# Releasing the row scatters of two slots together, behind one TensorE product

## The chip, the cores and the metric

The kernel runs on one core of a Trainium2 chip. The metric is the device time of one execution in microseconds (us). The core has five engines, each with its own in-order instruction stream: TensorE (PE; its weight loads are listed as PEld), VectorE (DVE), ScalarE (ACT), GpSimd (POOL) and SyncE (SP, which here only issues DMAs). They wait for one another through semaphores. Every DMA, whoever issues it, runs on the same 16 DMA engines.

## The reference

One layer of message passing on a graph of 6,250 nodes and 100,000 edges, 128 features each. For every edge, the features of its source node, of its destination node and of the edge itself go through one linear layer, a layer norm and a ReLU; the messages are summed per source node, added to the node's features, and the sum is normalised.

```python
row, col = (edge_index[0], edge_index[1])
msg_in = jnp.concatenate([x[row], x[col], edge_attr], axis=-1)
h = msg_in @ W + b
mu = jnp.mean(h, axis=-1, keepdims=True)
var = jnp.mean(jnp.square(h - mu), axis=-1, keepdims=True)
h = (h - mu) * jax.lax.rsqrt(var + LN_EPS) * gamma + beta
msg = jax.nn.relu(h)
out = jax.ops.segment_sum(msg, row, num_segments=x.shape[0])
# and outside: x = _layernorm(x + out)
```

Edges come sorted by destination. The sum goes by source, which is in no order.

## The kernel before, in words

The kernel sorts the edges by blocks of source nodes through device memory. The 100,000 edges are 782 tiles of 128, and four tiles are a **slot** (196 slots, numbered q). In each slot PE multiplies the edge features (L611) and adds the rows of the destination nodes, which it picks out of a small window with a one-hot matrix (L615). ACT moves the four finished tiles from PSUM into one of eight buffers `hs` (L623; slot q uses buffer q mod 8) and adds the source's number within its block (L624). POOL then writes the 128 rows of each tile to their places in a table `sorted` in device memory, with one indirect DMA per tile (L641): four **scatters** per slot, 782 in all.

The tiles are cut into six **splits** (42, 42, 42, 30, 20 and 20 slots), each with a table of its own. While the slots of one split run, the table of the split before is read back, two blocks of 125 nodes at a time (a **pair**, SP's loads `hl`, L715), and worked off in steps that are woven into the slots by a fixed flow (`FLOW`, `work`): DVE builds the one-hot matrix (`ohe`, L733), PE turns it (L745) and ACT copies it (L749), ACT seeds PSUM with the rows (L755), PE adds the source rows (L772), ACT squares and takes roots (L781, L784), DVE scales (L790, L796), PE sums by node (L805), DVE adds to the accumulator (L810). The last split has a loop of its own at the end (class `Unit`, loads L831, one-hot L838). Ahead of all this, some 42 slots also project the node features (L391 to L417), and `places` works out where each row goes.

The order of PE, DVE, ACT and SP is written out by hand. POOL has its own stream, which in this stage holds scatters alone. A slot's scatters are collected in the list `waiting`. Up to slot 12 and from slot 195 on they are issued untied, as soon as ACT has written the buffer. Between, `scatters(n, True)` is called in each slot and takes the n = 4 scatters of the slot before; `done` lists the products that PE was given since the last call with their costs (4 for an f32 product, 1 for a bf16 one), and the loop over `done` picks those at which 1/4, 2/4, 3/4 and 4/4 of the cost is reached. Scatter k waits by semaphore for product `at[k]`. So the four scatters of slot q - 1 go out along the products of slot q. Each scatter also waits until the scatter eight before it has landed, since there are eight semaphores for them.

What depends on a scatter: ACT's write of the same `hs` buffer eight slots later, and the first `hl` load of a split, some five slots after the split's last slot; for the last split that is the first load at L831.

Of the kernel before, what the change touches and what calls it, by code (L numbers as in the profile page):

```python
# [84 lines left out]
def fast_path(ctx, tc, io, bad_d, found):  # L85
# [10 lines left out]
    written = mybir.DependencyInfo(mybir.DependencyClass.Sync, mybir.DependencyReason.DATA)  # L96
# [91 lines left out]
    iota_p, zero_p, at = beside[:, 0:P], beside[:, P:P + 1], beside[:, P + 8:P + 8 + NB]  # L188
# [27 lines left out]
    def more_constants():  # L216
        nc.vector.tensor_copy(ident_f16, ident)
        nc.vector.tensor_scalar(minus_f16, ident, -1.0, None, op0=ALU.mult)
        nc.vector.tensor_scalar(twice_f16, ident, 2.0, None, op0=ALU.mult)
# [342 lines left out]
    def edge_loads(q):  # L562

        if q % DG or q >= PIECES:
            return
        t0 = q * PT
        g = min(DG, PIECES - q)
        if ("eT", q // DG) not in held:
            edge_feats(q)
        db = edge.tile([P, DG * PT * P], BF16, name="db", bufs=3)  # L570
        if q >= BY_PE:
            c1 = g * PT * P
            nc.sync.dma_start(
                db[:, :c1], dram_ap(drel_d, t0 * P, [[0, P], [1, c1]]))
        held[q // DG] = (held.pop(("eT", q // DG)), db)

    def edge_window(q):
        if q >= PIECES:
            return
        k = sum(q >= x for x in TABLE_FROM[1:])  # L580
        base = nc.values_load(base_c[0:1, q:q + 1], engines=[mybir.EngineType.SP],
                              min_val=0, max_val=TABLES[k][1] - TABLES[k][0] - WN,
                              skip_runtime_bounds_check_because="kept inside the table")
        win = edge.tile([P, D], BF16, name="win", bufs=6)
        i = nc.sync.dma_start(win[:3 * WN, :], xb_d[k][:, bass.ds(base, WN), :])
        held["win", q] = win
        return i

    def edge_hot(q):
        if q >= PIECES:  # L590
            return
        m = min(PT, TILES - q * PT)
        c0 = q % DG * PT * P
        db = held[q // DG][1][:, c0:c0 + m * P]
        if q < BY_PE:
            db = psum.tile([P, PT * P], F32, name="sel", bufs=BANKS["sel"])
            nc.tensor.matmul(db, ones_h[0:1, :], drel0[0:1, q, :], start=True, stop=True)
        oh = edge.tile([P, PT * P], BF16, name="ohd", bufs=3)
        nc.vector.tensor_scalar(oh[:, :m * P], db, part_w, None, op0=ALU.is_equal)  # L599
        held["oh", q] = oh  # L600

    def edges(s, q):
        t0 = q * PT
        m = min(PT, TILES - t0)
        c0 = q % DG * PT * P
        eT = held[q // DG][0][:, c0:c0 + m * P]
        oh, win = held.pop(("oh", q)), held.pop(("win", q))
        hp = psum.tile([P, PT, P], F32, name="hp", bufs=2)
        for j in range(m):
            at = slice(j * P, (j + 1) * P)  # L610
            pe(nc.tensor.matmul(hp[:, j, :], eT[:, at], w[:, 2, :], start=j == 0, stop=False,  # L611
                                skip_group_check=True), 4)
        for j in range(m):
            at = slice(j * P, (j + 1) * P)
            pe(nc.tensor.matmul(hp[:, j, :], oh[:3 * WN, at], win[:3 * WN, :],  # L615
                                start=False, stop=j == m - 1, skip_group_check=True))
        held["hp", q] = hp

    def evict(s, q):
        t0 = q * PT  # L620
        m = min(PT, TILES - t0)
        hs, hp = hs_all[q % HS], held.pop(("hp", q))
        nc.scalar.copy(hs[:, :m, 0:D], hp[:, :m, :])  # L623
        nc.scalar.copy(hs[:, :m, D], sloc[:, t0:t0 + m])  # L624
        waiting.extend((s, q, j) for j in range(m))

    TIE = (12, 195)
    waiting = []

    def scatters(n, tied):  # L630

        total, seen, at = sum(c for _, c in done), 0, []
        for i, c in done:
            seen += c
            while len(at) < n and seen * n >= (len(at) + 1) * total:
                at.append(i)
        done.clear()
        for k, (s, q, j) in enumerate(waiting[:n]):
            t = q * PT + j
            parts = P if t < TILES - 1 else LAST  # L640
            i = nc.gpsimd.indirect_dma_start(  # L641
                out=sorted_d[s][:, :],
                out_offset=bass.IndirectOffsetOnAxis(ap=place_i[:parts, t:t + 1], axis=0),
                in_=hs_all[q % HS][:parts, j, :], in_offset=None,
            )
            if tied:
                tc.add_manual_dep(i.ins, at[k].name, written, reason="rows behind products")
            tc.declare_no_dep(i.ins, group=f"scatter{s}", reason="rows of different edges")
            tc.add_to_no_dep_group(f"scatter{s}", i.ins)
            if q < EARLY:  # L650
                tc.declare_no_dep(i.ins, group="clear", reason="see check_early")
                tc.add_to_no_dep_group("early", i.ins)
        del waiting[:n]
# [305 lines left out]
    def run(g, n=1):  # L959
        for _ in range(n):  # L960
            next(g, None)
# [114 lines left out]
    def work(n):  # L1076

        nonlocal n_steps
        for _ in range(n):
            for off, step in FLOW:  # L1080
                i = n_steps - LEAD - off
                if i % 4 or not 0 <= i // 4 < len(pairs):
                    continue
                if step is None:
                    load_pair(*pairs[i // 4])
                    continue
                if off == 0:
                    at_work[i // 4] = Pair(*pairs[i // 4])
                step(at_work[i // 4])
            n_steps += 1  # L1090
# [7 lines left out]
    def steps_due(q):  # L1098
        for (q0, n0), (q1, n1) in zip(due, due[1:]):
            if q0 <= q < q1:  # L1100
                return n0 + (n1 - n0) * (q - q0) // (q1 - q0)
        return 0
# [3 lines left out]
    def clear_pairs(s, n):  # L1106
        for p0 in range(cleared[s], min(cleared[s] + n, NB // 2)):
            i = clear(s, p0, 1, nc.sync)
            if s == 0:
                tc.declare_no_dep(i.ins, group="early", reason="see check_early")  # L1110
                tc.add_to_no_dep_group("clear", i.ins)
            cleared[s] = p0 + 1

    ahead = 3
    for s, (n_tiles, _, _, _) in enumerate(SPLITS):
        p0, p1 = first_tile[s] // PT, -(-first_tile[s + 1] // PT)
        slots = p1 - p0
        for i in range(slots):
            q = p0 + i
            for g in groups:  # L1120
                run(g)
            if q == 1:
                more_constants()

            while ahead <= min(q + 4, 3 + q + q // 3):
                edge_loads(ahead)
                edge_window(ahead)
                ahead += 1
            if s + 1 < n_split and i >= slots - (30 if s else 26):
                clear_pairs(s + 1, 1 if slots > NB // 2 else 2)  # L1130
            edge_hot(q + 2)
            edges(s, q)
            for g in groups:
                run(g)
            n = steps_due(q + 1) - n_steps
            work(min(n, 1))
            evict(s, q)
            if not TIE[0] <= q < TIE[1]:
                scatters(len(waiting), False)
            for g in steps_at.pop(q, []):  # L1140
                run(g)
            work(n - 1)
            if TIE[0] < q < TIE[1]:
                scatters(len(waiting) - PT, True)
            if s == 0:
                if todo and q % 4 != 3:
                    groups = groups[-5:] + [project(*todo.pop(0))]
                    run(groups[-1])
                    if n_todo - len(todo) in loads:
                        load_x(*loads.pop(n_todo - len(todo)))  # L1150
                clear_pairs(0, 1 + i % 2 if 1 <= i else 0)
            if q in x_at:
                acc_load(x_at[q])
            if q in others:
                others.pop(q)()
            if q in s_at:
                acc_scale(*s_at[q])
        if s == 0:
            assert not todo and not loads
# [344 lines left out]
```

## Time and profile before

| | |
|---|---|
| three runs, median (lowest to highest) | 1376.14 us (1372.72 to 1377.86) |
| the profiled execution's own time | 1380.69 us |
| its span, first to last instruction | 1378.9 us |
| mean granted TensorE clock | 0.857 |
| moved by DMA | 247.22 MB, 179 GB/s on average |

The span and what lies around it (1.8 us) make the profiled execution's time; it is 4.55 us above the median of the runs. An engine's busy time is the union of its instructions; "issue" as a releaser means that the profile shows nothing that the engine waited for, and "remote" that a semaphore ended the wait at a time at which the profile shows no instruction's end that would have set it.

### The profile page before, as it was taken

Reading aid. Unit: us, or ns where it says so; the run is one execution under the profiler, and the core shown is the slowest. Engines: PE = TensorE matmul, PEld = TensorE weight load, DVE = VectorE, ACT = ScalarE, POOL = GpSimd, SP = SyncE. Lnnn points to the kernel's source line nnn. Section 1 sums busy time; section 2 is a strip of 40 time slices with the busy share of each in tenths; the row PEclk is TensorE's granted clock in tenths of the full one; section 3 lists DMA queues with packets and bytes.
Section 4 is the critical chain, followed back from the end, with each engine's and each line's share of the span. In section 5 each row is a group of like instructions: output and inputs, shape, how many; then the busy total and the mean of one; then the engine's idle time right before and its main releaser. Section 6 shows DMA issues by size and latency. Waiting matters only on the chain. (4 is left out here: it accounts for less than half of the span.)

```text
span 1378.9 us, 27543 instructions
## 1 busy us (share of the span) xinstructions
PE 975.2 (71%) x8886; PEld 870.3 (63%) x8886; DVE 855.0 (62%) x2376; ACT 773.5 (56%) x3118; POOL 798.9 (58%) x835
## 2 busy tenths in 40 slices
PE   7457464345767676778777677778778787876895
PEld 5445453334666665777676667777778776765674
DVE  8573434524465656556575657678688867554797
ACT  4223232112555655564565557676778788665796
POOL 3656666666566665666565666566555555556054
PEclk9768687666888989878888899999999999988898
DMA  7758586455666655556656555665667655543332
GB/s 223 236 168 255 171 241 204 142 154 155 184 199 210 199 158 163 178 157 198 207 171 200 172 184 178 208 208 187 190 193 227 183 181 171 170 140 100 112 122 72
DMA packets 128052, 247.22 MB, mean 179 GB/s; under 512 B 47005, under 2 KB 61231, under 8 KB 127897
## 3 DMA queue, kind: packets, MB, share of 16 engines
q1 hardware_dynamic: 101924, 191.92, 46.8%
q0 software_dynamic: 25104, 53.05, 11.0%
q8 instruction: 71, 1.16, 0.4%
q14 instruction: 83, 0.68, 0.2%
q10 hardware_dynamic: 870, 0.40, 0.1%
HBM read 155.49 MB, written 89.80 MB: 178 GB/s over the span
## 5 line engine op out<-in xcount | busy, mean ns | idle before, releaser
L641 POOL DMA_INDIRECT sorted<-hs,place_i x782 | 760.4, 972 | 498.1 <-issue 210.6
L772 PE MATMUL sel<-xa,ohn 128*128 128x128 bf16 x2550 | 214.3, 232 | 174.9 <-issue 78.5
L781 ACT ACTIVATE sq<-sel 128x128 f32<-128x128 f32 x850 | 224.2, 280 | 158.9 <-PE sel L772 58.2
L772 PEld LDWEIGHTS <-ohn 128*128 128x128 bf16 x2550 | 174.8, 104 | 204.4 <-issue 174.7
L611 PE MATMUL hp<-w,eT 128*128 128x128 f32 x1564 | 258.3, 314 | 51.2 <-issue 37.9
L611 PEld LDWEIGHTS hp<-w,eT 128*128 128x128 f32 x1564 | 234.3, 225 | 83.2 <-issue 59.3
L805 PE MATMUL pa<-msg,ohe 128*128 128x130 f32 x1700 | 259.2, 308 | 24.1 <-issue 14.9
L623 ACT COPY hs<-hp 128x512 f32<-128x512 f32 x196 | 114.2, 583 | 288.7 <-issue 97.7
L805 PEld LDWEIGHTS pa<-msg,ohe 128*128 128x128 f32 x1700 | 236.4, 217 | 32.2 <-issue 19.0
L796 DVE SCALAR_TENSOR_TENSOR msg<-sel,rstd,cut 128x128 f32<-128x128 f32 x850 | 240.7, 345 | 8.0
L781 ACT ACTIVATION_READ_ACCUMULATOR sq<-sel 128x1 f32 x850 | 178.8, 210 | 0.0
L810 DVE TENSOR_TENSOR acc<-acc,pa 128x260 f32<-128x260 f32 x125 | 53.0, 424 | 201.0 <-PE pa L805 57.9
L733 DVE TENSOR_TENSOR ohe<-hl,beside 128x1024 f32<-128x1024 f32 (+2 forms) x125 | 131.4, 1052 | 23.3 <-PE sel L772 14.6
L749 ACT COPY ohn<-tr 128x1024 bf16<-128x1024 bf16 (+2 forms) x125 | 109.5, 876 | 37.9 <-PE pa L805 14.7
L755 ACT COPY sel<-hl 128x512 f32<-128x512 f32 (+1 forms) x225 | 127.9, 569 | 1.8 <-DVE msg L796 1.0
L599 DVE TENSOR_SCALAR ohd<-db,part_w 128x512 bf16<-128x512 bf16 x192 | 69.7, 363 | 72.1 <-remote 50.9
L615 PE MATMUL hp<-win,ohd 126*128 126x128 bf16 x782 | 88.5, 236 | 17.4 <-issue 15.4
L790 DVE RECIPROCAL rstd<-std 128x4 f32<-128x4 f32 (+1 forms) x225 | 38.6, 171 | 96.7 <-ACT std L784 45.2
L615 PEld LDWEIGHTS <-ohd 126*128 126x128 bf16 x782 | 69.0, 108 | 25.2 <-issue 20.9
L745 PE MATMUL tr<-ident_h,ohe 128*128 128x128 bf16 x850 | 75.5, 230 | 11.1 <-issue 9.4
L784 ACT ACTIVATE std<-ss,eps 128x4 f32<-128x4 f32 (+1 forms) x225 | 66.9, 297 | 7.3
L745 PEld LDWEIGHTS <-ohe 128*128 128x128 bf16 x850 | 57.7, 103 | 14.3 <-issue 14.2
(198 smaller groups left out, 1043.4 us busy)
## 6 DMA issues: line engine op xcount, KB each, us to landing
eT<-in_eT SPq DMA_DIRECT2D x96, 512.0 KB
hl<-sorted SPq DMA_DIRECT2D x75, 528.0 KB
db<-drel_d SPq DMA_DIRECT2D x96, 256.0 KB
sorted<-empty SPq DMA_DIRECT2D x100, 198.0 KB
hl<-sorted SPq DMA_DIRECT2D x50, 264.0 KB
sorted<-hs,place_i POOLq DMA_INDIRECT x782
hl<-sorted SPq DMA_DIRECT2D x25, 396.0 KB
sorted<-empty SPq DMA_DIRECT2D x50, 132.0 KB
```

Source lines behind the costliest of these rows:

```text
L611: pe(nc.tensor.matmul(hp[:, j, :], eT[:, at], w[:, 2, :], start=j == 0, stop=False, skip_group_check=True), 4)
L615: pe(nc.tensor.matmul(hp[:, j, :], oh[:3 * WN, at], win[:3 * WN, :], start=False, stop=j == m - 1, skip_group_check=True))
L623: nc.scalar.copy(hs[:, :m, 0:D], hp[:, :m, :])
L641: i = nc.gpsimd.indirect_dma_start(out=sorted_d[s][:, :], out_offset=bass.IndirectOffsetOnAxis(ap=place_i[:parts, t:t + 1], axis=0), in_=h ...
L733: nc.vector.tensor_tensor(self.ohe[:, :k, :], self.hl[:, :k, D:D + 1].to_broadcast([P, k, P]), row_bc(iota_p, k), op=ALU.is_equal)
L745: pe(nc.tensor.transpose(tr[:, j, :], half[:, j0 + j, 1::2], ident_h))
L749: nc.scalar.copy(self.ohn[:, :self.k, :], self.tr[:, :self.k, :])
L755: nc.scalar.copy(self.sel[g][:, :m, :], self.hl[:, j0:j0 + m, 0:D])
L772: pe(nc.tensor.matmul(sel[:, j, :], self.ohn[:, j0 + j, :], xa[:, b, i * D:(i + 1) * D], start=False, stop=j == m - 1 and i == 2, skip_gro ...
L781: nc.scalar.activation(sq[:, j, :], self.sel[g][:, j, :], AF.Square, accum_out=ss[:, j:j + 1])
L796: nc.vector.scalar_tensor_tensor(self.msg[:, j0 + j, 0:D], self.sel[g][:, j, :], rstd[:, j:j + 1], cut, op0=ALU.mult, op1=ALU.max)
L805: pe(nc.tensor.matmul(self.pa[:, h, :], self.ohe[:, j, :], self.msg[:, j, :], start=(j == h), stop=(j == k - 2 + h)), 4)
```

## The change

Two lines. The call in the slots' loop is made in odd slots alone, so that it finds eight tiles in `waiting` beside the newest four (in slot 13, the first, there are four). In odd slot q it issues the scatters of slots q - 2 and q - 1, and `done` covers the products of slots q - 1 and q. And every scatter of a call waits for `at[-1]`, the last of these products, which is the last product of slot q; `at[k]` is no longer used.

```diff
             if tied:
-                tc.add_manual_dep(i.ins, at[k].name, written, reason="rows behind products")
+                tc.add_manual_dep(i.ins, at[-1].name, written, reason="rows behind products")
...
             work(n - 1)
-            if TIE[0] < q < TIE[1]:
+            if TIE[0] < q < TIE[1] and q % 2:
                 scatters(len(waiting) - PT, True)
```

The instructions and their order are the same on all five engines; the waits of POOL's scatters differ. At the end, slot 194 is even, so slot 193's four scatters, which were tied in slot 194, now go out untied in slot 195 with those of slots 194 and 195: ten in place of six.

## The prediction

> **What bounds the kernel now.** I read the page first, for the busy shares.
>
> ```profile
> span 1378.9 us, 27543 instructions
> PE 975.2 (71%) x8886; PEld 870.3 (63%) x8886; DVE 855.0 (62%) x2376; ACT 773.5 (56%) x3118; POOL 798.9 (58%) x835
> L641 POOL DMA_INDIRECT sorted<-hs,place_i x782 | 760.4, 972 | 498.1 <-issue 210.6
> ```
>
> No engine is full; PE is the fullest. POOL is at a scatter for over half the span, 0.97 us each. The next view is the table by stage: the slots with projections, three stretches of tied slots, and the tail, where no scatter is left. Its columns are the stretch, its length, busy us (and instructions) of PE, PEld, DVE, ACT and POOL, then the granted clock, the DMA share and GB/s.
>
> ```profile
> 100.00:340.00 240.00, 123.68 (x806) 107.37 (x806) 96.78 (x194) 57.67 (x139) 152.14 (x158) 0.72 0.62 188
> 340.00:640.00 300.00, 222.81 (x2042) 203.58 (x2042) 180.03 (x474) 172.88 (x696) 183.92 (x190) 0.86 0.59 184
> 640.00:930.00 290.00, 220.96 (x2097) 198.47 (x2096) 187.35 (x496) 180.60 (x739) 175.67 (x181) 0.87 0.62 191
> 930.00:1265.00 335.00, 263.11 (x2810) 247.25 (x2809) 236.68 (x696) 249.15 (x1064) 190.91 (x197) 0.94 0.58 177
> 1286.00:1340.00 54.00, 51.75 (x497) 40.15 (x496) 48.30 (x172) 46.11 (x237) 17.31 (x17) 1.00 0.41 132
> ```
>
> Where no scatter runs PE is busy 51.75 / 54 = 0.96 of the time at the full clock. In the three tied stretches together it is busy (222.81 + 220.96 + 263.11) / 925 = 0.764, and in the first row 0.515. What are the others waiting for? The table of waits, for 340 to 1265 us (total us, times, longest):
>
> ```profile
> PEld L772 <- issue: 169.6, 181, 5.4
> POOL sorted L641 <- issue: 133.0, 356, 3.1
> POOL sorted L641 <- PE pa L805: 64.6, 53, 3.0
> DVE acc L810 <- remote: 48.1, 15, 9.8
> ACT sq L781 <- remote: 43.5, 18, 5.1
> ACT hs L623 <- remote: 33.5, 12, 3.9
> ```
>
> DVE and ACT wait 125 us in these three rows for something that the profile can't tie to an instruction's end, and all three wait for products of PE. PE's weight loads sit 170 us with nothing to wait for. One place shows both at once, in the timeline of slots 42 to 44 (start, length, instruction, idle time before it):
>
> ```profile
> 283.85 0.39 PE L615 MATMUL hp<-win,ohd 126*128 126x128 bf16 x4
> 284.28 0.97 POOL L641 DMA_INDIRECT sorted<-hs,place_i  x1 [0.30 <-issue]
> 293.20 0.97 POOL L641 DMA_INDIRECT sorted<-hs,place_i  x1 [0.30 <-issue]
> 295.38 0.35 DVE L599 TENSOR_SCALAR ohd<-db,part_w 128x512 bf16<-128x512 bf16 x1 [12.70 <-remote]
> 296.06 0.58 PE L611 MATMUL hp<-w,eT 128*128 128x128 f32 x1 [11.83 <-issue]
> ```
>
> PE's last product is shown to end at 284.24; DVE gets its word of PE at 295.38, and PE goes on at 296.06. Between the two POOL rows lie six more of the same kind, 0.30 us apart: an unbroken train of scatters, and PE's signal comes through 1.2 us after its last one (293.20 + 0.97). I read this as: **while scatters follow each other without a pause, PE's completions reach the others late**, and PE's own issue stalls with them.
>
> To see whether the length of a train matters, I cut 340 to 1262 us at each pause of POOL over 0.36 us: a stretch goes from the start of one train to the start of the next. First the 33 stretches whose train has five scatters or more (first, last, sum), then the 159 with one to three (first and sum), then the sum of the 17 with four.
>
> ```profile
> 358.30:370.50 12.20, 7.85 (x65) 6.03 (x64) 2.36 (x9) 4.40 (x17) 7.78 (x9) 0.89 0.80 252
> 922.90:930.50 7.60, 5.48 (x63) 4.92 (x62) 4.08 (x14) 6.51 (x26) 4.97 (x5) 1.00 0.73 244
> sum 263.50, PE 178.71 PEld 156.24 DVE 162.25 ACT 141.46 POOL 167.57; mean PE 5.42 PEld 4.73 DVE 4.92 ACT 4.29 POOL 5.08
> ...
> 353.40:355.20 1.80, 1.80 (x16) 1.79 (x15) 0.00 (x0) 1.80 (x4) 0.97 (x1) 0.81 0.91 228
> sum 544.00, PE 447.07 PEld 417.62 DVE 361.44 ACT 394.86 POOL 310.74; mean PE 2.81 PEld 2.63 DVE 2.27 ACT 2.48 POOL 1.95
> ...
> sum 108.00, PE 75.25 PEld 69.99 DVE 74.71 ACT 62.57 POOL 66.08; mean PE 4.43 PEld 4.12 DVE 4.39 ACT 3.68 POOL 3.89
> ```
>
> PE is busy 0.82 of the time around short trains, 0.70 around trains of four, 0.68 around longer ones (447.07 / 544, 75.25 / 108, 178.71 / 263.5). The waits for PE's products are what breaks the trains up: POOL waits 64.6 us for L805 alone.
>
> **The change, part by part.** Nothing is added to or removed from an engine, so every term is one of order.
>
> *The trains.* The eight scatters of a call wait for one product, so once the first goes, the other seven follow: 8 x (0.97 + 0.30) = 10.2 us without a pause, then nothing until the next odd slot's end. The three tied rows hold 190 + 181 + 197 = 568 scatters, 71 calls of eight, one each 925 / 71 = 13.03 us, with 706.88 / 71 = 9.96 us of PE work each. Now price one cycle. During the train PE is busy at some share; what is left of the 9.96 us is done in the pause.
>
> - Train at 0.678 (trains of five or more) and pause at 0.958 (no scatter, the tail's row): 6.92 us done in the train, 3.04 / 0.958 = 3.17 us after it, 13.37 us a cycle. That is 0.34 us more, 71 x 0.34 = +24 us.
> - The pause no better than around short trains, 0.822: 3.04 / 0.822 = 3.70, 13.90 us a cycle, +62 us.
> - Train at today's mean, 0.764, pause at 0.958: 7.79 and 2.26 us, 12.46 us a cycle, -40 us. So there is a gain to be had: all scatters of two slots packed leave 2 to 3 us that nothing disturbs.
> - Train at the share of the first stage, 0.515, where POOL's trains are mostly of eight and more: 5.25 and 4.92 us, 15.17 us a cycle, +152 us.
>
> I take the first. A train of eight is nearest to the longest ones seen in the same work, and the pause has no scatter in it, as the tail. The point from which the sign turns is (9.96 - 0.958 x (13.03 - 10.2)) / 10.2 = 0.71.
>
> [...]
>
> *The first stage* (slots 13 to 42, to about 275 us). POOL already runs there in long trains: 158 scatters in 240 us leave it 1.52 us each, of which 1.27 are used. I take 0, with ends of -10 and +15 us: two slots there are 8 x 1.52 = 12.2 us, in which a fixed train of 10.2 us can gain or lose about half a microsecond like the cycle above, some 15 times, and a little more where POOL falls behind.
>
> *Later scatters, and who needs them.* A tile now waits up to two slots (13 us) and then up to 10.2 us more. ACT needs the buffer eight slots later, 8 x 6.5 = 52 us, so no ACT write waits. A split's first load comes five slots, 33 us, after its last slot; the last scatter is done by about 23 us. Both at 0; if that cover were gone, SP would hold its whole queue, the edge features too, for the time missing.
>
> *The end.* Here the cover is thin.
>
> ```profile
> 1261.73 0.97 POOL L641 DMA_INDIRECT sorted<-hs,place_i  x1 [1.33 <-PE pa L805]
> 1274.57 0.87 POOL L641 DMA_INDIRECT sorted<-hs,place_i  x1 [0.30 <-issue]
> 1281.71 9.40 SPq L831 DMA_DIRECT2D hl<-sorted  x7
> 1289.91 0.68 DVE L838 TENSOR_TENSOR ohe<-hl,beside 128x512 f32<-128x512 f32 x1
> ```
>
> The product at 1261.7 is slot 193's last. From there POOL has eight tied and ten untied scatters, 18 x 1.27 = 22.9 us, and is done at 1284.6 in place of 1275.4. The first L831 load needs them landed (1.2 us, as above): 1285.8, 4.1 us later than now. DVE wants its data at 1289.91 and does other work until then without a gap, so 0, at most +4 us; behind the waiting load SP has only the next L831 loads.
>
> The sum: 1378.9 + 1.8 around the span + 24 = 1404.7 us for the profiled execution. The median of the runs shown is 4.6 us below that execution, so 1400 us.
>
> **The rivals.**
>
> *Packing pays* (faster). The stall is set by how much of the time scatters run, not by the train's length, and long trains are a result: after a stall PE runs through several release points at once. For it: in the stretches with long trains, time per scatter is no longer than elsewhere (7.6 us for five). Against: 0.82, 0.70 and 0.68 in the same work. With today's mean in the train the price is -40 us: 1336 us, and up to 1368 as the share nears 0.71, from where it decides.
>
> *Nothing moves* (the change does not do what it says to the time). What holds PE up is other traffic, for instance the edge and `hl` loads, at a DMA share of 0.6 in all three tied rows, and the scatters only happen beside it. [...] Against: the 12.70 us wait, whose stretch has PE waiting with POOL alone at work for the first half. 1376 us.
>
> *A train of eight starves PE* (much slower). No product gets its word through for most of 10.2 us, as in the wait of 12.70 us and as in the first stage's 0.515. For it: these two; against: there PE, ACT and DVE hand each other single banks, so each late signal counts fully, and the tied stretches have two groups in flight. 1376 + 152 = 1528 us at the end; half of it, 1450, if the share is 0.60.
>
> **How the numbers follow.** The forecast (train at 0.65 to 0.70, 1385 to 1438 us) gets 0.45, packing pays 0.25, nothing moves 0.16, starving 0.14. Faster and slower count from 0.5%, about what a measurement of this kernel can tell from no change. Slower: the forecast and starving, less 0.01 for the forecast's edge, 0.58; within: 0.16; faster: 0.25 and that edge, 0.26. The likeliest case's own range is 1385 to 1438 us. With cases of both signs the range goes from 1345 us (inside the packing case, 0.08 below it) to 1465 us (inside starving, 0.10 above).
>
> **What would show it.** POOL in blocks of eight at 1.27 us with one pause a cycle, from slot 15 on, and no wait between the eight. The table by stage: PE's share in the three tied stages below 0.764 is the forecast, above it the packing case. PE's share inside the trains is the deciding number: under 0.71 slower, over it faster, under 0.6 starving. The waits "remote" of DVE and ACT should rise and lie inside the trains, and PE's idle time should leave the pauses. L831's first load should move some 4 us against the last tied slot, with no gap of DVE ahead of L838. The forecast is wrong if the trains are there and PE's share in them is that of short trains, or if the pauses go unused because ACT or DVE are behind then.

## The result, and the profile after

The changed kernel took 1617.89 us in the median of four runs (1611.89 to 1622.34), the kernel before 1374.43 us beside it: a ratio of 1.178 (1.175 to 1.182). The sign of the prediction was right, the size was not: +243 us where it had +24.

The page of the changed kernel (profiled execution 1611.89 us): the span, the busy times, the granted clock in 40 slices, and the group of the scatters.

```profile
span 1610.1 us, 26994 instructions
PE 1092.8 (68%) x8886; PEld 955.0 (59%) x8886; DVE 854.8 (53%) x2376; ACT 770.0 (48%) x3118; POOL 795.2 (49%) x835
PEclk8787675677778777878777778877887787778798
L641 POOL DMA_INDIRECT sorted<-hs,place_i x782 | 756.8, 968 | 732.4 <-issue 242.8
```

DVE, ACT and POOL work as long as before, to a few us. PE does the same 8886 products and is busy 117.6 us longer (975.2 before), at a mean granted clock of 0.777 where it was 0.857. The other half of the span's 231.2 us is idle time of PE, 113.6 us more.

Where? I cut both executions at the first product of slots 54, 100, 146 and 194 (the tied slots without projections lie between the first and the last cut). Windows of the changed kernel, columns as in the prediction, then the three middle ones of the kernel before:

```profile
0.00:328.20 328.20, 177.64 (x1141) 150.16 (x1141) 163.15 (x372) 86.05 (x201) 199.75 (x222) 0.73 0.66 200
328.20:676.20 348.00, 246.94 (x1997) 217.93 (x1996) 174.45 (x461) 169.19 (x683) 178.36 (x185) 0.78 0.50 157
676.20:1036.90 360.70, 258.27 (x2146) 226.78 (x2146) 194.29 (x516) 184.65 (x755) 178.00 (x184) 0.78 0.50 155
1036.90:1486.30 449.40, 319.74 (x2769) 289.30 (x2767) 233.46 (x685) 243.94 (x1049) 188.79 (x196) 0.78 0.42 131
1486.30:1610.10 123.80, 90.22 (x842) 70.88 (x840) 89.46 (x345) 86.17 (x432) 50.31 (x50) 0.89 0.30 98
```

```profile
339.40:633.90 294.50, 217.31 (x1997) 198.15 (x1997) 175.07 (x462) 169.31 (x681) 179.68 (x185) 0.86 0.58 182
633.90:930.40 296.50, 227.31 (x2151) 204.75 (x2147) 192.91 (x512) 185.14 (x756) 180.25 (x185) 0.87 0.62 192
930.40:1261.30 330.90, 259.18 (x2768) 243.53 (x2766) 234.42 (x689) 247.66 (x1060) 188.34 (x194) 0.94 0.58 178
```

The first 54 slots (0 to 339.4 us before, 0 to 328.2 us now) are 11.2 us shorter, the end is 6.2 us longer, and the 140 slots between carry the loss: 53.5, 64.2 and 118.5 us, most in the stage that had the highest clock. They took 921.9 us for 70 pairs of slots, 13.17 us each, and take 1158.1 us now, 16.54 us each.

The waits of the changed kernel (total us, times, longest), for the whole span:

```profile
DVE acc L810 <- remote: 228.8, 36, 11.4
ACT sq L781 <- remote: 157.4, 28, 8.7
ACT hs L623 <- remote: 140.6, 24, 10.9
```

526.8 us in these three. In the kernel before they are 159.5 us over the whole span, and the prediction had counted the 125 us of them that lie in the tied stages. One cycle shows what they are. Windows of 1.27 us from the start of one train of eight (347.88 us) to the start of the next, three of them left out:

```profile
347.88:349.15 1.27, 1.27 (x21) 1.26 (x21) 1.06 (x2) 1.24 (x10) 0.96 (x1) 1.00 0.41 97
...
350.42:351.69 1.27, 1.27 (x14) 1.27 (x13) 0.38 (x2) 0.98 (x2) 0.96 (x1) 1.00 0.84 249
351.69:352.96 1.27, 0.96 (x7) 0.41 (x5) 0.00 (x0) 0.59 (x5) 0.97 (x1) 1.00 0.59 233
352.96:354.23 1.27, 0.41 (x2) 0.19 (x2) 0.00 (x0) 0.84 (x6) 0.97 (x1) 1.00 0.17 57
354.23:355.50 1.27, 0.29 (x1) 0.11 (x2) 0.00 (x0) 0.00 (x0) 0.97 (x1) 1.00 0.18 60
...
356.77:358.04 1.27, 0.29 (x3) 0.10 (x1) 0.00 (x0) 0.00 (x0) 0.97 (x1) 0.59 0.16 53
358.04:359.31 1.27, 0.94 (x4) 0.38 (x4) 0.00 (x0) 0.00 (x0) 0.00 (x0) 0.50 0.16 53
...
360.58:361.85 1.27, 1.27 (x10) 0.89 (x9) 1.16 (x5) 0.08 (x1) 0.00 (x0) 0.50 0.89 324
361.85:363.12 1.27, 1.27 (x15) 1.27 (x13) 1.27 (x2) 0.12 (x1) 0.00 (x0) 0.50 0.93 299
363.12:364.57 1.45, 1.45 (x15) 1.45 (x14) 1.11 (x7) 1.42 (x10) 0.00 (x1) 0.75 0.45 116
```

PE runs on for three scatters. Its products (the number in brackets behind its busy time) are 21 and 14 in the windows of the first and third, then 7, 2 and 1; DVE and then ACT stand still; and the DMA share is down to 0.17: the DMA engines are mostly idle while PE stalls. When the train is over PE comes back, but the clock that it is granted (third column from the right) has gone from 1.00 to 0.50, and the pause that was to make up for the train is run at half speed.

The timeline of another train shows the stall at its finest, a product every 0.7 us with nothing to wait for, and DVE's word of PE 1.9 us behind the last scatter (610.19 + 0.97):

```profile
608.70 0.22 PE L772 MATMUL sel<-xa,ohn 128*128 128x128 bf16 x1 [0.50 <-issue]
609.42 0.22 PE L772 MATMUL sel<-xa,ohn 128*128 128x128 bf16 x1 [0.49 <-issue]
610.14 0.22 PE L772 MATMUL sel<-xa,ohn 128*128 128x128 bf16 x1 [0.51 <-issue]
610.19 0.97 POOL L641 DMA_INDIRECT sorted<-hs,place_i  x1 [0.30 <-issue]
613.04 0.43 DVE L810 TENSOR_TENSOR acc<-acc,pa 128x260 f32<-128x260 f32 x1 [8.47 <-remote]
```

The trace's records of semaphore updates show the lateness directly, and that it is PE's alone. From 328.2 to 1486.3 us, 371 of the 728 recorded updates of PE's semaphore lie more than 0.3 us behind the last product before them that raises it; of DVE's 845 and ACT's 668 none lies that far behind its instruction. Over the whole trace, in the first scatter of a train PE's lie 0.01 us behind at the median, in the fifth 0.8 us, in the eighth 2.6 us; from 4 us behind a train on it is 0.01 us again.

### The profile page after: what moved, and what is told of

The parts are those of the page before. It is cut to its first block, busy times and chain, and to the rows that moved or that the text cites. A ratio compares the mean times of both kernels' runs of the same rounds, so it can differ in the third digit from the quotient of the medians.

```text
span 1610.1 us, 26994 instructions
## 1 busy us (share of the span) xinstructions
PE 1092.8 (68%) x8886; PEld 955.0 (59%) x8886; DVE 854.8 (53%) x2376; ACT 770.0 (48%) x3118; POOL 795.2 (49%) x835
## 5 line engine op out<-in xcount | busy, mean ns | idle before, releaser
L611 PE MATMUL hp<-w,eT 128*128 128x128 f32 x1564 | 285.4, 327 | 104.2 <-issue 72.1
L805 PE MATMUL pa<-msg,ohe 128*128 128x130 f32 x1700 | 299.4, 335 | 59.6 <-issue 40.9
L772 PE MATMUL sel<-xa,ohn 128*128 128x128 bf16 x2550 | 241.7, 249 | 143.0 <-issue 98.9
L611 PEld LDWEIGHTS hp<-w,eT 128*128 128x128 f32 x1564 | 251.6, 235 | 136.3 <-issue 98.7
L805 PEld LDWEIGHTS pa<-msg,ohe 128*128 128x128 f32 x1700 | 272.8, 243 | 73.2 <-issue 58.8
L772 PEld LDWEIGHTS <-ohn 128*128 128x128 bf16 x2550 | 198.1, 113 | 172.6 <-issue 141.8
L810 DVE TENSOR_TENSOR acc<-acc,pa 128x260 f32<-128x260 f32 x125 | 53.0, 424 | 412.9 <-remote 228.8
L745 PE MATMUL tr<-ident_h,ohe 128*128 128x128 bf16 x850 | 90.0, 244 | 39.9 <-issue 37.1
L615 PE MATMUL hp<-win,ohd 126*128 126x128 bf16 x782 | 94.2, 246 | 29.7 <-issue 28.2
L745 PEld LDWEIGHTS <-ohe 128*128 128x128 bf16 x850 | 64.8, 111 | 51.4 <-issue 49.2
```

What stands on the lines that cost most here:

```text
L745: pe(nc.tensor.transpose(tr[:, j, :], half[:, j0 + j, 1::2], ident_h))
L772: pe(nc.tensor.matmul(sel[:, j, :], self.ohn[:, j0 + j, :], xa[:, b, i * D:(i + 1) * D], start=False, stop=j == m - 1 and i == 2, skip_gro ...
L805: pe(nc.tensor.matmul(self.pa[:, h, :], self.ohe[:, j, :], self.msg[:, j, :], start=(j == h), stop=(j == k - 2 + h)), 4)
```

## The experiments

One thing has to be said ahead: each batch of runs below is compared with the kernel before on the same chip, and that kernel took 1357 to 1374 us in some batches and 1120 us in others, the same within a batch; one chip showed 1119.55 us in one batch and 1356.77 us in a later one. In the batches at 1120 us the loss of the changed kernel that is studied here does not appear. Thirteen of the eighteen runs met 1120 us and say only what their kernels cost without it.

The theories that the expectations name: A, PE's loss comes with the length of an unbroken train, from its fourth scatter on; B, it comes from holding all scatters for one late product; C, it comes from taking two slots together, whose rows are then late; D, it comes from the bytes that the scatters write; E, trains cost on any chip. Beside these, a busy POOL alone could do it.

| kernel | this, us | before beside it, us | ratio (95%) |
|---|---|---|---|
| e6 the changed kernel again | 1619.26 | 1373.04 | 1.181 (1.176 to 1.185) |
| e11 four behind the last product | 1433.93 | 1373.65 | 1.043 (1.035 to 1.051) |
| e14 eight, spread | 1355.48 | 1356.77 | 0.999 (0.996 to 1.002) |
| e15 eight, with a pause in the middle | 1403.42 | 1356.77 | 1.033 (1.027 to 1.039) |
| e16 before, with a pause behind every second | 1356.61 | 1356.77 | 0.998 (0.996 to 1.001) |
| e1, e7 four behind the last product | 1128.80, 1126.54 | 1119.55, 1119.75 | 1.009, 1.007 |
| e2, e8 eight, spread | 1119.20, 1119.46 | 1119.55, 1119.75 | 1.000, 1.000 |
| e4, e9, e19 rows of 16 bytes | 1119.06, 1118.96, 1118.94 | 1119.55, 1119.75, 1119.37 | 0.999, 1.000, 1.001 |
| e5, e10, e12 no tied scatter | 1108.68, 1110.53, 1109.99 | 1119.55, 1119.75, 1120.39 | 0.990, 0.992, 0.990 |
| e18 eight behind the middle product | 1127.24 | 1119.51 | 1.007 |
| e17, e20 sixteen | 1148.32, 1147.36 | 1119.51, 1119.37 | 1.025, 1.024 |

**The two halves of the change, the bytes, and POOL's being busy.** e1 makes only the first half of the diff, e2 only the second. e4 and e5 don't read the sorted rows back; they load as much from the edge features instead.

```diff
e1: -tc.add_manual_dep(i.ins, at[k].name, written, ...)
    +tc.add_manual_dep(i.ins, at[-1].name, written, ...)
e2: -if TIE[0] < q < TIE[1]:
    +if TIE[0] < q < TIE[1] and q % 2:
e4 (on the changed kernel):
    -out=sorted_d[s][:, :],  in_=hs_all[q % HS][:parts, j, :]
    +out=narrow_d[s][:, :] if tied else ...,  in_=hs_all[q % HS][:parts, j, 0:4 if tied else ROW]
    (both hl loads) -dram_ap(sorted_d[s], ...)   +io["eT"][:, p * k * ROW:(p + 1) * k * ROW]
e5 (on the changed kernel, with the same hl loads):
    +if tied:
    +    i = nc.gpsimd.tensor_tensor(busy, busy, busy, op=ALU.mult)
    +    tc.add_manual_dep(i.ins, at[-1].name, written, ...)
    +    continue
```

> Only the first half of the change: every slot, four scatters, all behind the last product. Theory A (what costs is the length of a train: in the changed kernel PE's share of the time, in steps of 1.27 us from a train's start, is 0.98, 0.95, 0.89, 0.75, then 0.50, 0.34, 0.30, 0.37): trains of four lose about 1.27 x (0.02 + 0.05 + 0.11 + 0.25) = 0.5 us plus about 0.7 us for the step after the last, 1.2 us for a slot of 5.0 us of PE work, 6.2 us against 6.5 now: 1330 to 1420 us. Theory B (what costs is that all scatters are held for one late point and then meet the next slot's start): the loss is there with four as with eight, 1550 us or more.

> Only the second half of the change: eight scatters of two slots in one call, but each behind its own product, spread over the products of two slots. Theory A: no train is forced, so about the kernel before, 1340 to 1410 us. Theory C (what costs is that rows of two slots wait together and come later, for the buffers and for the loads behind them): 1500 us or more.

> The changed kernel, where each tied scatter writes 16 bytes of each row, not 528, to a table of its own; the sorted rows are then loaded from the edge features instead, in the same sizes. The number of rows and of instructions stays. Theory A, by the scatter as an instruction with its 128 rows: trains of eight and PE's share in them stay, 1560 to 1640 us. Theory D (the bytes that the scatters write fill a path that others need): the loss goes in proportion to the bytes, 1376 us or less.

> The changed kernel, where each tied scatter is replaced by an elementwise product of 128 x 512 on POOL, some 1.04 us as the 128 x 512 products of the tail take there, behind the same product of PE; the sorted rows are loaded from the edge features. Trains of eight on POOL stay, without any transfer. Theory A with the cause in the scatter's transfer or its making: PE's share rises to 0.95 nearly everywhere, 1376 - 240 or so, 1130 to 1250 us. If POOL's being busy is what delays PE's signals: 1500 us or more.

All four came out within 1% of a kernel before that took 1119.55 us, so they met no loss to tell apart. What they do show is the same program without it. The page of e2, and the largest of its waits:

```profile
span 1117.7 us, 27542 instructions
PE 876.6 (78%) x8886; PEld 806.5 (72%) x8886; DVE 848.5 (76%) x2376; ACT 765.8 (69%) x3118; POOL 796.5 (71%) x835
```

```profile
ACT hs L623 <- DMA sorted<-hs,place_i: 127.6, 50, 7.1
```

None of its waits is "remote", PE needs 876.6 us for its products at a granted clock of 0.911, and POOL goes from scatter to scatter with no more than the usual 0.30 us between, hundreds in a row, and sets the pace itself: ACT waits 127.6 us for it to empty a buffer. In the trace's records of semaphores PE's signal is 0.01 us behind its product there, within such a train too (one of 1633 is more than 0.3 us behind). So an unbroken train of scatters does not hold PE's signals up in every batch.

**The changed kernel again.**

> The changed kernel itself, unchanged, on the chip that this job gets. The kernel before took 1119.55 us on the chip of the first four experiments, not 1374, and PE's signals were 0.01 us late there with 632 scatters in one train. Theory A' (scatters hold up PE's signals on one chip and not on another): where the kernel before takes about 1120 us the changed one takes 1120 to 1140 us, with POOL's scatters as the limit in both; where the kernel before takes about 1374 us it takes 1600 to 1635 us. Theory E (trains of eight cost by themselves, whatever the chip): 1.10 times the kernel before or more on either.

This batch met a kernel before at 1373.04 us, and the ratio of the first measurement came back, 1.181. Theory E falls by e17 and e18 below: eight and sixteen at a time cost 0.7% and 2.5% where the kernel before takes 1120 us. The kernels of the first batch then ran again, e7 to e10 in one batch, e11 and e12 each in its own:

> The kernel of e1_last4 once more (four scatters a slot, all behind the last product), for a chip where the kernel before takes about 1374 us. Theory A (the length of a train decides): in the changed kernel on such a chip PE's share in steps of 1.27 us from a train's start is 0.98, 0.95, 0.89, 0.75, 0.50, 0.34, 0.30, 0.37; a train of four ends before the bad steps and loses about 0.5 us, and about 0.7 us in the step behind it, 6.2 us a slot against 6.5: 1330 to 1420 us. Theory B (all scatters held for one late point): 1500 us or more. Where the kernel before takes about 1120 us it says nothing more than e1_last4.

> The kernel of e2_two_spread once more (eight in a call, spread over the products of two slots), for a chip where the kernel before takes about 1374 us. Theory A: no train is forced, 1340 to 1410 us. Theory C (the pairing of slots, with rows that come later): 1500 us or more.

> The kernel of e4_rows16 once more (the changed kernel with 16 bytes written for each row, not 528), for a chip where the kernel before takes about 1374 us. If the scatter's making on POOL is what holds PE up: trains of eight with PE at 0.30 to 0.50 from the fifth step on, 1560 to 1640 us. If it is the bytes written: 1400 us or less, and no fall of PE's share within a train.

> The kernel of e5_no_dma once more (each tied scatter of the changed kernel replaced by a product of 128 x 512 on POOL, 1.04 us, which makes no transfer), for a chip where the kernel before takes about 1374 us. It took 1108.68 us on the chip where the kernel before takes 1120 us. If scatters hold PE up: within 2% of that, 1090 to 1130 us. If a busy POOL does: 1500 us or more. If this chip is slower in something besides: between 1130 and 1350 us.

> The kernel of e1_last4 a third time (four scatters a slot, all behind the last product); the first two times the kernel before took 1120 us on the chip, and nothing could be learned of the loss. Where the kernel before takes about 1374 us: theory A (the length of a train decides; a train of four ends before the steps in which PE's share falls to 0.50 and below) says 1330 to 1420 us, theory B (all scatters held for one late point) 1500 us or more. Where it takes about 1120 us: 1125 to 1132 us again.

> The kernel of e5_no_dma a third time (each tied scatter of the changed kernel replaced by a product of 128 x 512 on POOL, 1.04 us, behind the same product of PE; the sorted rows are loaded from the edge features), for a chip where the kernel before takes about 1374 us and the changed one 1618 us. Where the kernel before takes 1120 us it took 1109 to 1111 us. If scatters are what holds PE up: 1090 to 1130 us, POOL in trains all the same. If a busy POOL does: 1500 us or more. If the chip is slower in something besides: between 1130 and 1350 us.

Only e11 met it. Four scatters behind the last product cost 60 us (1.043), nearer to theory A's 1420 than to theory B's 1500, and outside both. Its windows say why. First the sums over its 74 trains of just four scatters between 335 and 1300 us (from the first start to 0.3 us behind the last end), then those over its 31 trains of eight:

```profile
sum 376.71, PE 314.43 PEld 293.89 DVE 259.99 ACT 286.62 POOL 286.79; mean PE 4.25 PEld 3.97 DVE 3.51 ACT 3.87 POOL 3.88
...
sum 315.10, PE 195.92 PEld 170.65 DVE 186.39 ACT 151.02 POOL 239.62; mean PE 6.32 PEld 5.50 DVE 6.01 ACT 4.87 POOL 7.73
```

A train of four leaves PE 314.43 / 376.71 = 0.83 of the time; where two fours met, it is 195.92 / 315.10 = 0.62. Most of PE's idle time within these trains lies in the eights that form by themselves: 119.18 us in 31 of them, 62.28 us in the 74 fours.

**The length of a train, with the late product kept.** e14 is e2 once more. e15 leaves the changed kernel's eight behind one late product and only breaks them, with work of POOL's own; e16 breaks the trains of the kernel before.

```diff
e15 (on the changed kernel), behind the tie:
+k == 3 and tc.add_manual_dep(nc.gpsimd.tensor_tensor(busy, busy, busy, op=ALU.mult).ins, at[-1].name, ...)
e16 (on the kernel before), behind the tie:
+k % 2 and tc.add_manual_dep(nc.gpsimd.tensor_tensor(*[busy[:, :128]] * 3, op=ALU.mult).ins, at[k].name, ...)
```

> The kernel of e2_two_spread again (eight in a call, each behind its own product, spread over the products of two slots). Where the kernel before takes about 1374 us: theory A (trains) 1340 to 1410 us, as no train is forced; theory C (two slots' rows come later) 1500 us or more. Where it takes about 1120 us: the same as before, as e2_two_spread showed.

> The changed kernel with a pause in each train of eight: behind the fourth scatter POOL multiplies 128 x 1024 numbers of no use, about 2.0 us at the rate of the 128 x 512 products. POOL is busy through 12.4 of the 13.0 us of a cycle. Where the kernel before takes about 1374 us: theory A (the length of a train of scatters decides) gives trains of four twice, about the 1434 us of e11_last4, 1400 to 1470 us; theory B or C (one late product, two slots at once) leaves 1580 us or more; a busy POOL that holds PE up gives more than 1618 us. Where it takes about 1120 us POOL is the limit and 91 pauses of about 2.1 us come on top: 1250 to 1320 us.

> The kernel before with a short pause behind every second tied scatter: POOL multiplies 128 x 128 numbers of no use, about 0.4 us. No train is longer than two without a pause of 0.7 us or so; POOL needs 4 x 1.27 + 2 x 0.45 = 6.0 us of a slot's 6.5. Where the kernel before takes about 1374 us: if a short pause lets PE's signals through, PE stays near the 0.87 of the first steps of a train, 5.0 / 0.87 = 5.7 us, and POOL's 6.0 us a slot decide, 1290 to 1340 us; if the pause is too short to matter, 1360 to 1420 us. Where it takes about 1120 us, POOL is the limit and 362 pauses of 0.45 us come on top: 1220 to 1290 us.

All three met the loss. Taking two slots together costs nothing when their scatters are spread (0.999): theory C falls. A pause in the middle of each train, 2.1 us in the timeline, takes the ratio to the kernel before from 1.18 (in the batches at 1373 and 1374 us) to 1.033, and its 1403.42 us lie in theory A's range. Theory B falls, since all eight still wait for the last product, and so does POOL's being busy as such, since POOL works 967.9 us there and 795.2 us in the changed kernel. The sums over the trains of e15, 81 of four and 30 of eight (two fours that met):

```profile
sum 410.85, PE 352.11 PEld 328.07 DVE 296.89 ACT 314.50 POOL 323.77; mean PE 4.35 PEld 4.05 DVE 3.67 ACT 3.88 POOL 4.00
...
sum 304.75, PE 196.26 PEld 174.38 DVE 176.48 ACT 142.03 POOL 239.78; mean PE 6.54 PEld 5.81 DVE 5.88 ACT 4.73 POOL 7.99
```

Again 0.86 and 0.64. e16 did not gain: 1356.61 us, next to the 1360 us and more that were expected of a pause too short to matter. Nearly all its scatters come one or two at a time, with at least 0.60 us behind every second one, and yet 550 of the 1108 recorded updates of PE's semaphore between 340 and 1262 us lie more than 0.3 us behind, as in the kernel before (594 of 1101). So the count of scatters in an unbroken train is not the whole measure: a gap of 0.60 us is not enough, the 2.1 us of e15 take most of the loss away, and where between them the limit lies was not measured. Neither e14 nor e16 beats the kernel before.

**Twice the length, and another place.** Sixteen at a time (`q % 4 == 3` for `q % 2`), and eight behind the fourth of the eight spread products (`at[3]` for `at[-1]`):

> The changed kernel with sixteen scatters at every fourth slot, all behind the last product of the four slots. Theory A, by the shares of the changed kernel's steps: a train of 20.3 us leaves PE 1.27 x (0.98 + 0.95 + 0.89 + 0.75 + 0.50) + 14.0 x 0.35 = 10.1 us of work, of the 2 x 11.6 us of four slots 13.1 us are left for the pause at 0.83, 15.8 us; 36.1 us for four slots against 2 x 16.3, 46 x 3.5 = 160 us more than the changed kernel: 1700 to 1820 us where the kernel before takes 1357 to 1374 us. If only the number of bursts or their place counts: 1620 us or less.

> The changed kernel with its eight scatters behind the fourth of the eight spread products, the middle of the two slots, not behind the last. Trains of eight as before, half a cycle earlier. Theory A (the train's length decides, wherever it starts): 1570 to 1650 us where the kernel before takes 1357 to 1374 us. Theory B (the late product and the start of the next slot): 1500 us or less.

> The kernel of e4_rows16 once more (the changed kernel with 16 bytes written for each row of a tied scatter, not 528; the sorted rows are loaded from the edge features). Where the kernel before takes 1357 to 1374 us: if the scatter as an instruction with its 128 rows holds PE up, 1560 to 1640 us, with PE's share under 0.55 from the fifth step of a train; if it is the bytes, 1400 us or less. Where the kernel before takes about 1120 us: 1119 us again.

> The kernel of e17_four_slots once more (sixteen scatters at every fourth slot). Where the kernel before takes 1357 to 1374 us: theory A by PE's share at each step of a train 1700 to 1820 us; if only the number of bursts or their place counts 1620 us or less. Where the kernel before takes about 1120 us: 1148 us again.

All four met a kernel before at 1120 us. Without the loss, holding eight back costs 0.7% and sixteen 2.5%; the changed kernel itself met no such batch, and about 1% is an estimate for it from e1 and e18. What sixteen do with the loss, what is left of it without any tied scatter, and whether the bytes or the making of a scatter cause it, was not measured and stays open.

## Why the prediction was wrong, point by point

**The trains: right.** POOL runs blocks of eight at 1.27 us with a pause between, 69 of exactly eight from 328 to 1480 us. **The cause: right as far as it was tested.** PE's signals come later and later within a train (0.01 us behind in the first scatter, 2.6 us in the eighth), PE stalls with nothing to wait for, and breaking the train for 2.1 us takes most of the loss away (e15, 1.033 where the changed kernel has 1.18), while neither the pairing of slots (e14, 0.999) nor more work on POOL (e15, 967.9 us) brings it. How a scatter holds PE's signals up is not shown.

**The price of a cycle: wrong, in three terms, the largest one unlooked for.** The prediction had 13.37 us: 6.92 us of PE's 9.96 us of work within the train (share 0.678), and 3.04 us of it behind the train at 0.958. The sums over the 69 trains of the changed kernel, over the pauses behind them, and over both:

```profile
sum 701.82, PE 448.57 PEld 390.32 DVE 331.51 ACT 290.16 POOL 533.79; mean PE 6.50 PEld 5.66 DVE 4.80 ACT 4.21 POOL 7.74
...
sum 435.50, PE 361.08 PEld 329.64 DVE 252.49 ACT 297.14 POOL 0.08; mean PE 5.23 PEld 4.78 DVE 3.66 ACT 4.31 POOL 0.00
...
sum 1137.32, PE 809.65 PEld 719.96 DVE 584.00 ACT 587.30 POOL 533.87; mean PE 11.73 PEld 10.43 DVE 8.46 ACT 8.51 POOL 7.74
```

A cycle is 1137.32 / 69 = 16.48 us, 3.11 us over the forecast. Step by step from 13.37 us:

- The train's share is 448.57 / 701.82 = 0.639, not 0.678: 0.42 us of work more for the pause, at 0.958 0.44 us. The 0.678 was taken over trains of five or more together with the pauses behind them; those trains alone have 158.28 / 219.83 = 0.72, and trains of eight fall further.
- PE's work is 11.73 us a cycle, not 9.96: 1.77 / 0.958 = **1.85 us**. The prediction took 9.96 us as fixed. It is the same products at a lower granted clock: in the three tied stages busy time times clock is 187, 198 and 244 us before and 193, 201 and 249 us after. The trace of before held this: the first stage stands at a clock of 0.72 beside 1.00 in the tail, and the prediction's table quotes both.
- The pause gives 361.08 / 435.50 = 0.829, not 0.958: 5.23 / 0.829 against 5.23 / 0.958, 0.85 us. It opens with 1 to 2 us in which PE is still slow (the windows at 358.04 above). The kernel before had the same opening: its 33 pauses behind trains of five or more, 1.3 us each, have PE at 20.42 / 43.75 = 0.47. The prediction had a pause at 0.822 as its second case.

Behind the clock stands the length of the stall, as far as the two traces show it. The clock records hold 1.00 and 0.50 alone, and all but the last of each trace are 3.41 us long or a multiple of it; at 0.50 it stands for 395 us in the kernel before and for 719 us in the changed one, where from 328 to 1480 us it falls 71 times, once a cycle, for 6.8 us at the median, with PE busy 0.35 of the 4 us ahead; in the kernel before, from 340 to 1262 us, it falls 39 times for 3.4 us. Cut into stretches of 3.41 us, the records at 1.00 within these limits part by PE's share: in the changed kernel it is 0.33 at the median and 0.58 at most in the 70 stretches just ahead of a fall, and 0.56 or more in the 118 others; in the kernel before 0.34 and at most 0.54 in 40, and 0.47 or more in the 173 others. In the last 3.41 us of each record at 0.50 PE is busy 0.77 or more, in both kernels. In the cycle above PE is below half from 352.96 us, the clock stands at 0.50 from 357.01 us on, and it is back at 363.84 us. Within a train of four (e11) PE is idle for (376.71 - 314.43) / 74 = 0.84 us, so that one such train leaves it 1 - 0.84 / 3.41 = 0.75 of a stretch, an estimate that lies above all those ahead of a fall; and the mean clock of e11 (0.842) and e15 (0.854) is close to that of before (0.857), where the changed kernel has 0.777.

**The deciding number was ill chosen.** The prediction named PE's mean share within the train, with 0.6 as the mark below which PE starves. It is 0.639 and PE starves, because the mean mixes good steps with bad ones: over the 69 trains the eight steps have 0.98, 0.95, 0.89, 0.75, 0.51, 0.36, 0.31 and 0.36. By steps of 1.27 us the trains of five or more in the kernel before already showed it; here the sums over their first six steps, 33 trains:

```profile
sum 41.89, PE 39.41 PEld 38.40 DVE 36.97 ACT 39.19 POOL 31.98; mean PE 1.19 PEld 1.16 DVE 1.12 ACT 1.19 POOL 0.97
sum 41.91, PE 39.03 PEld 37.02 DVE 36.60 ACT 31.73 POOL 32.57; mean PE 1.18 PEld 1.12 DVE 1.11 ACT 0.96 POOL 0.99
sum 41.90, PE 35.26 PEld 30.93 DVE 33.08 ACT 31.17 POOL 32.05; mean PE 1.07 PEld 0.94 DVE 1.00 ACT 0.94 POOL 0.97
sum 41.90, PE 22.00 PEld 17.00 DVE 27.83 ACT 17.81 POOL 32.10; mean PE 0.67 PEld 0.52 DVE 0.84 ACT 0.54 POOL 0.97
sum 41.90, PE 19.17 PEld 13.54 DVE 16.33 ACT 9.00 POOL 32.09; mean PE 0.58 PEld 0.41 DVE 0.49 ACT 0.27 POOL 0.97
sum 39.42, PE 16.01 PEld 12.76 DVE 7.27 ACT 8.54 POOL 4.87; mean PE 0.50 PEld 0.40 DVE 0.23 ACT 0.27 POOL 0.15
```

0.94, 0.93, 0.84, then 0.53, 0.46, 0.41; the sixth lies mostly behind the trains' ends (POOL 4.87 us). A train of eight, with 0.40 for the two steps that these do not show, leaves 1.27 x 4.9 = 6.2 us of work; with 9.96 us and a pause at 0.958 that makes 14.1 us a cycle, some +75 us over 71 cycles: three times the forecast, and still a third of the truth, for want of the clock.

**The first stage:** 0 with ends of -10 and +15 us; it is 11.2 us shorter up to slot 54, just past the lower end, and the cause of that stays open. **Later scatters:** no cost seen; ACT's waits for a scatter's landing are 13.1 us in the whole span (34.7 us before). **The end:** 0 to +4 us, measured +6.2. The mechanism was another: DVE still reaches L838 without waiting for its data, but the eighteen scatters, a train of four and 1.3 us later one of fourteen, hold PE's signals up, and DVE waits 11.38 us at L810 in the timeline, until 2.8 us after the longer one's end, where it waited 7.93 us. The prediction's 1.2 us between the last scatter and the first L831 load was the lag of a PE signal, not of a landing; the load is issued 6.3 us behind the last scatter before and 6.8 us now.

**The rivals.** "Packing pays" and "Nothing moves" fell. "A train of eight starves PE" was the right one, given 0.14 and 1528 us; its price was taken from the first stage's share and lacked the longer work, and its cycle adds up to 10.2 + 4.92 = 15.12 us, +148 us, not to 15.17 and +152. Against "Nothing moves" stand the windows of the cycle above, where PE stalls at a DMA share of 0.16 to 0.18, with little other traffic left to hold it up. In e2, at 1120 us, none of the waits is "remote", and in its batch taking all tied scatters away (e5) is worth 1% (1108.68 us against 1119.55).

## What to carry to other kernels

When a stall builds up, don't price it by its mean over a stretch: lay the stretches on top of each other and read the share step by step, since a change that makes them longer adds only the last steps (here 0.51, 0.36, 0.31 and 0.36 behind four that start at 0.98, with a mean of 0.639). PE's busy time was no constant of the work here: the same 8886 products took 975.2 us before and 1092.8 us now, as a stall of some 4 us a cycle was paid a second time, in the clock (a mean of 0.777 where it was 0.857; 0.854 with the trains broken in e15). That speaks for short interruptions rather than one long. And where several scatters are to be released, spread the releases: in the batches with the loss, eight in a row cost 18%, four and four with 2 us between 3%, and the spread eight of e14 nothing.

## What the runs showed of the hardware that was not expected

The same kernel takes 1120 us or 1357 to 1374 us, from batch to batch, on one chip both; its runs within a batch agree within 1.2%. The difference goes with PE's signals: where the kernel before takes 1120 us, those of e2 are on time within trains of hundreds of scatters; where it takes 1357 us or more, half of them are late. One more thing differs: the traces at 1120 us hold 26,200 to 26,900 records of semaphore updates for kernels with all scatters, those at 1357 us and above 10,000 to 11,100, the kernel before among them. Whether whatever loses records also delays signals was not tested, and nothing in these runs says what sets the one or the other. Every run on record carries a granted clock, which is read from a trace, so none was made without tracing, and whether the loss would be there without it is not known.
